# Last scan layer: D*x moved from TensorE to VectorE, three steps reordered, activation functions applied to whole tiles

## The chip, the cores and the metric

The kernel runs on one core of one Trainium2 chip. Its time is the device time of one execution in microseconds (us); the median over several executions counts. Engines are named as the profile names them: PE (TensorE, matmuls), PEld (its weight loads), DVE (VectorE), ACT (ScalarE), POOL (GpSimd) and SP (SyncE, which issues the DMAs).

## What is computed

Four layers of selective scans ("Mamba") over images of 48 x 48 tokens with 192 channels, batch 4, and an MLP at the end. Only the last layer's scans change. The reference computes one scan in these lines:

```python
xz = jnp.einsum('nld,ed->nle', x, W_in)
xi, z = (xz[..., :di], xz[..., di:])
xc = conv_b + sum((xp[:, k:k + L, :] * conv_w[:, k] for k in range(K)))
xc = _silu(xc)
dbc = jnp.einsum('nld,ed->nle', xc, W_x)
dt = jax.nn.softplus(jnp.einsum('nlr,dr->nld', dbc[..., :dr], W_dt) + b_dt)
def step(h, inp):
    dt_t, B_t, C_t, x_t = inp
    h = jnp.exp(dt_t[:, :, None] * A) * h + (dt_t * x_t)[:, :, None] * B_t[:, None, :]
    return (h, jnp.einsum('nds,ns->nd', h, C_t))
...
y = jnp.swapaxes(ys, 0, 1) + D * xc
y = y * _silu(z)
return jnp.einsum('nld,od->nlo', y, W_out)
```

There are 384 inner channels (`di`) and 16 states (`ds`). The layer scans along the rows and along the columns of each image, each way forward and backward. All numbers are fp32.

## The kernel before

**Jobs, blocks, groups.** The last layer is 96 jobs (`RowJob`) in 48 pairs. A pair treats the same 384 tokens: the forward job first, then its twin, the backward job. A job has 3 blocks of 128 channels, a block has 4 groups of 4 states, so a job has 12 groups, and a pair 24. `run_jobs` walks over all 1152 groups in one loop; what it issues for one group `t` is called slot `t` here. Slots F0 to F11 are those in which the forward job is scanned, B0 to B11 those of the backward job. While a job is scanned, the next one is prepared: in F0 to F11 the backward twin, in B0 to B11 the forward job of the next pair.

**One group.** ScalarE makes four decays `a` by exponentials (`decay`, two groups ahead; the buffers of `a` are three). VectorE multiplies `du` by B for two of the four states (tile `inputs`), scans these two, and then scans the other two, whose inputs `made` TensorE has produced (`fill`, six products of the turned `du`, called `duT`, with diagonals that a DMA brings). There is one `made` tile, so the next `fill` can't begin before this second scan ends. POOL multiplies `h` by C (`weigh`), and TensorE, two groups later, sums the four states of `h` over the groups with transposing matmuls into the PSUM tile `y`, of which there is one (`reduce`). The order on TensorE, VectorE, ScalarE and POOL is the order of issue in the loop.

**Once per block.** POOL makes `dus` = delta * x (`drive`); TensorE turns it over (`turn`, two groups ahead of the block) and ScalarE copies the result to `duT`; ScalarE also copies `dus` to the PSUM tile `du` (`enter`, ahead of the last of four exponentials). When the block's sum is complete, ScalarE copies it to `yT` (`take`, three groups after the block's last), TensorE turns it back into a `ps` tile on top of the product diagD*x (`turn_back`, four groups after), ScalarE copies that to `yt`, and POOL multiplies it by the gate `z`. `take` therefore falls in slots 2, 6 and 10, `turn` too, `turn_back` in slots 3, 7 and 11, and `drive` in slots 1, 5 and 9.

**Preparing the next job.** `units` gives a list of units, each of a TensorE part and a ScalarE part, with the slots in which these are issued; `Stream.run` takes them in order, and the TensorE parts at most two ahead. For a forward job (in B slots): three input projections (0 to 2), three convolutions (3 to 5; each takes two `ps` tiles), the x-projection `bc` (6), whose result ScalarE copies to `bcd` and SP sends to DRAM and back as broadcasts (`spread`, `fetch`) and as diagonals `dg` by scattered writes, the deltas (8) and the gates z (9 to 11). For a backward job (in F slots): convolutions (0 to 2), `bc` (4), the deltas (6), and the output products of the pair before (7 to 10); where a prior result is added, POOL's addition and the store follow in slot 11. All these go through the pool `ps`, which has two PSUM tiles.

ScalarE holds one set of function tables at a time. Silu, softplus and the exponentials are in different sets here, so each change of function puts an ACT_TABLE_LOAD into its queue. Copies and additions of a bias need none.

Of the kernel before, what the change touches and what calls it, by code (L numbers as in the profile page):

```python
# [13 lines left out]
AF = mybir.ActivationFunctionType  # L14
ALU = mybir.AluOpType
# [7 lines left out]
CH = 384  # L23
# [307 lines left out]
class ScanJob:  # L331
# [16 lines left out]
    def turn_back(self, i):  # L348
        pass
# [29 lines left out]
    def projections(self, xs, *slots):  # L379

        k, nc, w, pools = self.k, self.k.nc, self.w, self.pools
        nr = 2 * N + w.rank
        W = pools.W

        def bc(px):
            self.bcd = k.tile(pools.two, [nr, W], "bcd", 1)
            if self.entry is not None:
                k.g.memset(self.bcd[:, self.entry : self.entry + 1], 0.0)
            k.copy(self.bcd[:, self.tokens], px)
            self.spread()  # L390

        def delta(i):
            def act(pd):
                if i == 0:
                    self.delta = k.tile(pools.two, [128, 3, CH], "delta")
                k.act(self.delta[:, i, :], pd, AF.Softplus, bias=w.dtb[:, i, :])

            return self.unit(
                slots[1],
                128,  # L400
                lambda ps: (ps, [(w.dtT[2 * N : nr, i, :], self.bcd[2 * N : nr, self.tokens])]),
                act,
            )

        first = self.unit(
            slots[0],
            nr,
            lambda ps: (ps, [(w.xpT[:, i, :], xs()[: pools.wide, i, :]) for i in range(3)]),
            bc,
        )  # L410
        return first, [delta(i) for i in range(3)]

    def spread(self):

        self.bc = self.k.dram([2 * N, self.pools.W], "bc")
        self.k.nc.sync.dma_start(self.bc, self.bcd[: 2 * N, :])

    def fetch(self, g):

# [111 lines left out]
class DirJob(ScanJob):  # L531
# [20 lines left out]
    def units(self, last):  # L552
        bc, deltas = self.projections(lambda: self.xs, (1, 1), (2, 2))
        return [bc, *deltas]
# [12 lines left out]
    def gate(self, i):  # L567

        self.ys = self.k.tile(self.pools.ps, [128, 512], "ps")[:64, :CH]
        self.k.mmo(self.ys, [(self.pools.sum, self.yc)])  # L570
# [186 lines left out]
class RowJob(MambaJob):  # L757
# [55 lines left out]
        self.duT[i] = k.tile(pools.two, [128, CH], "duT")  # L813
        k.copy(self.duT[i], ps)

    def turned_over(self, out, of, start=True):

        for b in range(3):
            at = slice(b * 128, (b + 1) * 128)
            ins = self.k.t.matmul(  # L820
                out[:, at],
                of[:, at],
                self.k.ident,
                start=start,
                stop=True,
                is_transpose=True,
                skip_group_check=True,
            )
        return ins
# [76 lines left out]
    def turn_back(self, i):  # L906

        k = self.k
        back = k.tile(self.pools.ps, [128, 512], "ps")[:, :CH]
        k.t.matmul(  # L910
            back,
            self.w.diagD[:, i, :],
            self.xs[:, i, :],
            start=True,
            stop=False,
            skip_group_check=True,
        )
        self.turned_over(back, self.turned, False)
        if i == 0:
            self.yt = k.tile(self.pools.one, [128, 3, CH], "yt", self.pools.yts)  # L920
        k.copy(self.yt[:, i, :], back)

    def convolved(self, step, *slots):

        k, pools, w = self.k, self.pools, self.w
        made = []
        both = [(n % 3, n // 3) for n in (2 * step, 2 * step + 1)]
        offs = [(w.taps - 1) + (w.taps - 1 - t) * (1 if self.rev else -1) for t in range(w.taps)]

        def pe():  # L930
            made.extend(k.tile(pools.ps, [128, 512], "ps")[:, :HALF] for _ in both)
            for t, off in enumerate(offs):
                for r in range(4):
                    rows = slice(r * 32, (r + 1) * 32)
                    for (i, n), ps in zip(both, made):
                        c = (r + i) % 4
                        x = self.xh[rows, i, n * RC // 2 : (n + 1) * RC // 2, off : off + S]
                        k.t.matmul(
                            self.shaped(ps[c * 32 : (c + 1) * 32]),
                            w.diag[rows, i, t, :],  # L940
                            x,
                            start=t == 0,
                            stop=t == w.taps - 1,
                        )

        def act():
            if step == 0:
                self.xs = k.tile(pools.two, [128, 3, CH], "xc", 3)
            for (i, n), ps in zip(both, made):
                at = slice(n * HALF, (n + 1) * HALF)  # L950
                k.act(self.xs[:, i, at], ps, AF.Identity, bias=w.cb[:, i, :])
            if step == 2:
                k.act(self.xs, self.xs, AF.Silu)

        return slots, pe, act

    def units(self, last):
        k, w, two = self.k, self.w, self.pools.two
        halo = w.taps - 1

        def project(e):
            return [(w.inT[:, m, e * 128 : (e + 1) * 128], self.u[:, m, :]) for m in range(2)]

        def inner(i, slot):
            return self.unit(
                (slot, slot),
                128,
                lambda ps: (ps, project(i)),
                lambda ps: k.copy(self.part(i, halo), self.shaped(ps)),
            )  # L970

        def gate(i, *slots):
            def act(ps):
                if i == 0:
                    self.z = k.tile(two, [128, 3, CH], "z")
                k.act(self.z[:, i, :], ps, AF.Silu)

            return self.unit(slots, 128, lambda ps: (ps, project(3 + i)), act)

        if self.twin is not None:  # L980
            self.z = self.twin.z
            outputs = last.outputs((7, 7), (8, 8), (9, 9), (10, 10), (11, 11)) if last else []
            bc, deltas = self.projections(lambda: self.xs, (4, 4), (6, 6))
            return [
                *(self.convolved(n, n, n) for n in range(3)),
                bc,
                *deltas,
                *outputs,
            ]
        bc, deltas = self.projections(lambda: self.xs, (6, 6), (8, 8))  # L990
        return [
            *(inner(n, n) for n in range(3)),
            *(self.convolved(n, 3 + n, 3 + n) for n in range(3)),
            bc,
            *deltas,
            gate(0, 9, 10),
            gate(1, 10, 10),
            gate(2, 11, 11),
        ]

    def outputs(self, *slots):
        k = self.k
# [106 lines left out]
def run_jobs(jobs, side=None):  # L1109
# [2 lines left out]


    behind = 2 if jobs[0].pools.rows else 1
    ahead, taken, gated, driven = 2, behind + 1, behind + 2, 3
    last_group = jobs[0].pools.groups - 1
    groups = [(job, i, g) for job in jobs for i in range(3) for g in range(last_group + 1)]
    per = len(groups) // len(jobs)
# [1 line left out]
    def at_group(t, g):  # L1120

        if 0 <= t < len(groups) and groups[t][2] == g:
            return groups[t][:2]
# [18 lines left out]
    for t in range(len(groups) + gated + 1):  # L1142
        n, at = divmod(t, per)
        if at == 0:
            last = jobs[n - 1] if n else None
# [7 lines left out]
        if t < len(groups):  # L1153
            job, i, g = groups[t]
            job.scan(i, g)
        coming = at_group(t + 1, 0)
        if t + ahead < len(groups):
            job, i, g = groups[t + ahead]
            job.decay(i, g, (lambda: coming[0].enter(coming[1])) if coming else None)
        if done := at_group(t - gated - 1, last_group):  # L1160
            done[0].close(done[1])
        if done := at_group(t - taken, last_group):
            done[0].take(done[1])
        if t < len(groups):
            if t + 1 < len(groups):
                job, i, g = groups[t + 1]
                job.carry(i, g)
            job, i, g = groups[t]
# [19 lines left out]
        if 0 <= t - behind < len(groups):  # L1188
            job, i, g = groups[t - behind]
            job.reduce(i, g)  # L1190
        if t + 1 < len(groups):
            job, i, g = groups[t + 1]
# [39 lines left out]
class MambaWeights(Weights):  # L1232
    def __init__(self, k, pool, inT, xpT, dtT, vec, tag):
        super().__init__(k, pool, 128, 12, xpT, dtT, vec, tag)
        self.k, self.pool, self.in_src = k, pool, inT
        self.D = self.vec[:, :, 17:18]
        self.cb = self.vec[:, :, 18:19]
        self.taps = vec.shape[1] - 19
        self.diagD = k.tile(pool, [128, 3, 128], f"diagD{tag}")
        self.unit = k.strip if self.taps == 4 else k.ident  # L1240
        self.diag = k.tile(pool, [128, 3, self.taps, self.unit.shape[1]], f"diag{tag}")

# [2 lines left out]

    def diagonals(self, i):

        self.scaled(self.diagD[:, i, :], self.k.ident, self.D[:, i, :])
        for t in range(self.taps):
            self.scaled(self.diag[:, i, t, :], self.unit, self.vec[:, i, 19 + t : 20 + t])  # L1250

# [979 lines left out]
```

## Time and profile before

| | us |
|---|---|
| median of 3 runs | 19079.52 |
| lowest, highest | 19050.35, 19124.85 |
| the profiled execution | 19116.63 |
| its span | 19114.80 |
| of it, the last layer's groups (12893 to 18655) | 5762 |

Busy in these 5762 us: PE 5321, DVE 5001, POOL 4592, ACT 4265, PEld 4318. Mean granted clock 0.98.

A group of the profile is a set of like instructions: engine, operation, output tile <- input tiles, partitions x elements, count, then busy us in total, mean ns of one, and the idle time ahead of them with what ended it. A wait row reads: who waited, for whom, us in total, times, longest. A timeline row gives start and duration in us, and in brackets the idle time ahead. Nearly all instructions of the scans carry line 59, which is a helper's; they are told apart by their tiles. Matmuls are counted in passes, two for an fp32 product, so `ps<-xc,diagD` x2 is one product.

### The profile page before, as it was taken

Reading aid. Unit: us, or ns where it says so; the run is one execution under the profiler, and the core shown is the slowest. Engines: PE = TensorE matmul, PEld = TensorE weight load, DVE = VectorE, ACT = ScalarE, POOL = GpSimd, SP = SyncE. Lnnn points to the kernel's source line nnn. Section 1 sums busy time; section 2 is a strip of 40 time slices with the busy share of each in tenths; the row PEclk is TensorE's granted clock in tenths of the full one; section 3 lists DMA queues with packets and bytes.
Section 4 is the critical chain, followed back from the end, with each engine's and each line's share of the span. In section 5 each row is a group of like instructions: output and inputs, shape, how many; then the busy total and the mean of one; then the engine's idle time right before and its main releaser. Section 6 shows DMA issues by size and latency. Waiting matters only on the chain. (4 is left out here: it accounts for less than half of the span.)

```text
span 19114.8 us, 243541 instructions
## 1 busy us (share of the span) xinstructions
PE 16743.5 (88%) x85680; PEld 9426.4 (49%) x85680; DVE 17183.8 (90%) x8452; ACT 13342.8 (70%) x24116; POOL 14745.6 (77%) x10861
## 2 busy tenths in 40 slices
PE   8999999999998877777877877879999999999999
PEld 4545545444444422222222222237777777777774
DVE  9999999999999599999999999968888888888883
ACT  6767767666665466777777777767777777777773
POOL 7888888878877188888888888858778787777780
PEclk9999999999999977888777788789999999999999
DMA  3333333323232266666666666653333333333331
GB/s 112 123 112 118 117 117 119 115 104 120 104 112 101 80 137 143 152 144 152 146 152 152 145 148 142 146 135 112 113 113 113 113 114 115 115 109 112 114 111 47
DMA packets 864867, 2316.13 MB, mean 121 GB/s; under 512 B 390520, under 2 KB 648160, under 8 KB 711200
## 3 DMA queue, kind: packets, MB, share of 16 engines
q1 hardware_dynamic: 863648, 2300.55, 43.3%
q8 instruction: 683, 11.19, 0.2%
q14 instruction: 536, 4.39, 0.1%
HBM read 2104.78 MB, written 196.65 MB: 120 GB/s over the span
## 5 line engine op out<-in xcount | busy, mean ns | idle before, releaser
L59 POOL TENSOR_TENSOR h<-h,bcb 128x1536 f32<-128x1536 f32 x3456 | 11916.5, 3448 | 1370.1 <-DVE h L59 919.4
L59 DVE TENSOR_TENSOR_SCAN h<-a,inputs 128x1540 f32<-128x1540 f32 (+1 forms) x3456 | 9764.1, 2825 | 146.7 <-DVE inputs L59 2.3
L104 ACT ACTIVATE a<-delta,A 128x384 f32<-128x384 f32 (+1 forms) x13824 | 7443.5, 602 | 1791.9 <-DVE h L59 1771.2
L59 DVE TENSOR_TENSOR inputs<-du,bcb 128x1540 f32<-128x1540 f32 (+1 forms) x3456 | 5185.7, 1500 | 463.2 <-ACT a L104 119.8
L59 PE MATMUL y<-h,ident 128*128 128x384 f32 x9216 | 3362.8, 511 | 131.0 <-POOL h L59 129.0
L59 PE MATMUL y<-h,sum 128*64 128x384 f32 x9216 | 2689.0, 647 | 730.9 <-POOL h L59 528.3
L59 PEld LDWEIGHTS y<-h,ident 128*128 128x128 f32 x9216 | 1796.3, 199 | 1605.0 <-POOL h L59 315.0
L59 DVE TENSOR_TENSOR_SCAN h<-a,made 128x768 f32<-128x768 f32 x1152 | 2005.3, 1741 | 637.6 <-PE made L59 637.1
L59 POOL COPY state<-h 128x4 f32<-128x4 f32 x2304 | 431.6, 187 | 1967.2 <-DVE h L59 1943.0
L59 PEld LDWEIGHTS y<-h,sum 128*64 128x64 f32 x9216 | 856.7, 168 | 2164.0 <-issue 977.2
L59 PE MATMUL made<-bcb,duT 128*128 128x128 f32 x13824 | 1797.7, 281 | 113.3 <-DVE h L59 110.2
L59 PE MATMUL y<-ident,h 128*128 128x128 f32 x13824 | 1787.1, 281 | 58.3 <-ACT yT L104 55.6
L59 PEld LDWEIGHTS made<-bcb,duT 128*128 128x128 f32 x13824 | 1682.7, 197 | 161.6 <-DVE h L59 157.5
L59 PEld LDWEIGHTS y<-ident,h 128*128 128x128 f32 x13824 | 1601.1, 145 | 305.3 <-issue 155.6
L59 PE MATMUL ps<-bcd,dtT 12*128 12x384 f32 (+1 forms) x2304 | 1122.6, 602 | 318.4 <-ACT delta L104 315.3
L59 PE MATMUL ps<-u,inT 96*128 96x384 f32 x3456 | 1266.4, 494 | 144.6 <-ACT z L104 100.7
L59 PE MATMUL ps<-xh,diag 32*32 32x192 f32 (+1 forms) x20160 | 1088.7, 339 | 140.7 <-ACT xc L104 131.7
L104 ACT ACT_TABLE_LOAD x793 | 1017.4, 1283 | 13.3
L101 ACT ACT_TABLE_LOAD x788 | 1011.0, 1283 | 14.2 <-PEq L2221 0.7
L59 PEld LDWEIGHTS ps<-u,inT 96*128 96x128 f32 x3456 | 633.7, 192 | 573.2 <-ACT z L104 159.2
L59 PEld LDWEIGHTS ps<-bcd,dtT 12*128 12x128 f32 (+1 forms) x2304 | 429.2, 213 | 924.9 <-ACT delta L104 559.5
L59 PEld LDWEIGHTS ps<-xh,diag 32*32 32x32 f32 (+1 forms) x20160 | 647.6, 110 | 478.8 <-ACT xc L104 190.1
(151 smaller groups left out, 14510.8 us busy)
## 6 DMA issues: line engine op xcount, KB each, us to landing
bcb<-bc SPq DMA_DIRECT2D x384, 1540.0 KB
bcb<-bc SPq DMA_DIRECT2D x768, 770.0 KB
bcb<-bc SPq DMA_DIRECT2D x384, 1152.0 KB
bcb<-dg SPq DMA_DIRECT2D x384, 384.0 KB
y<-o SPq DMA_DIRECT2D x192, 288.0 KB
xs<-xi_wh SPq DMA_DIRECT2D x96, 288.0 KB
xs<-xi_hw SPq DMA_DIRECT2D x96, 288.0 KB
added<-y SPq DMA_DIRECT2D x96, 288.0 KB
```

Of the source, the lines that this page charges most:

```text
L59: return lambda *a, **kw: self.tc.keep_in_program_order(op(*a, **kw))
L101: self.in_order(self.nc.scalar.preload_act_table_set(LOG_EXP))
L104: return self.in_order(self.nc.scalar.activation(out, in_, func, **kw))
```

## The change

- `turn_back` no longer multiplies by `diagD`; VectorE adds D*x while it takes the turned sum from PSUM, in place of ScalarE's copy. `diagD` isn't made for this layer.
- `drive` comes one slot earlier: `driven` is 4 in place of 3 (slots 0, 4, 8).
- `take` is issued ahead of `decay`'s exponentials instead of after them.
- The x-projection of a forward job moves from slot 6 to 7, the first gate's copy from 10 to 9, and the addition of the output from 11 to 10.
- The gates z are copied as they come, and one Silu over the three blocks follows in slot 2 of the forward job's run (after the twin's own Silu).
- The deltas are copied with their bias, and one softplus over the three blocks follows.

Layers before the last keep their code paths: `behind` is 1 there.

```diff
@@ delta (in projections): the activation becomes a method
+                lambda ps: self.softplus(i, ps),
...
@@ RowJob.turn_back
         back = k.tile(self.pools.ps, [128, 512], "ps")[:, :CH]
-        k.t.matmul(
-            back,
-            self.w.diagD[:, i, :],
-            self.xs[:, i, :],
-            start=True,
-            stop=False,
-            skip_group_check=True,
-        )
-        self.turned_over(back, self.turned, False)
+        self.turned_over(back, self.turned)
         if i == 0:
             self.yt = k.tile(self.pools.one, [128, 3, CH], "yt", self.pools.yts)
-        k.copy(self.yt[:, i, :], back)
+        k.v.scalar_tensor_tensor(
+            self.yt[:, i, :], self.xs[:, i, :], self.w.D[:, i, :], back, ALU.mult, ALU.add
+        )
@@ RowJob.convolved
             if step == 2:
                 k.act(self.xs, self.xs, AF.Silu)
+                if self.twin is not None:
+                    k.act(self.z, self.z, AF.Silu)
@@ RowJob.units
-                k.act(self.z[:, i, :], ps, AF.Silu)
+                k.copy(self.z[:, i, :], ps)
...
-            outputs = last.outputs((7, 7), (8, 8), (9, 9), (10, 10), (11, 11)) if last else []
+            outputs = last.outputs((7, 7), (8, 8), (9, 9), (10, 10), (10, 10)) if last else []
...
-        bc, deltas = self.projections(lambda: self.xs, (6, 6), (8, 8))
+        bc, deltas = self.projections(lambda: self.xs, (7, 7), (8, 8))
...
-            gate(0, 9, 10),
+            gate(0, 9, 9),
...
+    def softplus(self, i, pd):
+        k = self.k
+        if i == 0:
+            self.delta = k.tile(self.pools.two, [128, 3, CH], "delta")
+        k.act(self.delta[:, i, :], pd, AF.Identity, bias=self.w.dtb[:, i, :])
+        if i == 2:
+            k.act(self.delta, self.delta, AF.Softplus)
@@ run_jobs
-    ahead, taken, gated, driven = 2, behind + 1, behind + 2, 3
+    ahead, taken, gated, driven = 2, behind + 1, behind + 2, 2 + behind
...
             job.scan(i, g)
+        if behind == 2 and (done := at_group(t - taken, last_group)):
+            done[0].take(done[1])
         coming = at_group(t + 1, 0)
...
-        if done := at_group(t - taken, last_group):
+        if behind == 1 and (done := at_group(t - taken, last_group)):
             done[0].take(done[1])
```

More of the change, by code (lines that the diff above doesn't have):

```diff
@@ L392, in delta @@
         def delta(i):
[L393 to L396, printed above, removed]
             return self.unit(
@@ L401, in delta @@
                 lambda ps: (ps, [(w.dtT[2 * N : nr, i, :], self.bcd[2 * N : nr, self.tokens])]),
-                act,
+                lambda ps: self.softplus(i, ps),
             )
@@ L416, in spread @@
         self.k.nc.sync.dma_start(self.bc, self.bcd[: 2 * N, :])
+    def softplus(self, i, pd):
+        if i == 0:
+            self.delta = self.k.tile(self.pools.two, [128, 3, CH], "delta")
+        self.k.act(self.delta[:, i, :], pd, AF.Softplus, bias=self.w.dtb[:, i, :])
     def fetch(self, g):
@@ L814, in turn, with turned_over @@
         k.copy(self.duT[i], ps)
-    def turned_over(self, out, of, start=True):
+    def turned_over(self, out, of):
         for b in range(3):
@@ L823, in turned_over @@
                 self.k.ident,
-                start=start,
+                start=True,
                 stop=True,
@@ L999, in units, with softplus @@
         ]
+    def softplus(self, i, pd):
+        k = self.k
+        if i == 0:
+            self.delta = k.tile(self.pools.two, [128, 3, CH], "delta")
+        k.act(self.delta[:, i, :], pd, AF.Identity, bias=self.w.dtb[:, i, :])
+        if i == 2:
+            k.act(self.delta, self.delta, AF.Softplus)
     def outputs(self, *slots):
@@ L1238, in __init__ @@
         self.taps = vec.shape[1] - 19
-        self.diagD = k.tile(pool, [128, 3, 128], f"diagD{tag}")
+        if self.taps != 4:
+            self.diagD = k.tile(pool, [128, 3, 128], f"diagD{tag}")
         self.unit = k.strip if self.taps == 4 else k.ident
@@ L1246, in diagonals @@
     def diagonals(self, i):
-        self.scaled(self.diagD[:, i, :], self.k.ident, self.D[:, i, :])
+        if self.taps != 4:
+            self.scaled(self.diagD[:, i, :], self.k.ident, self.D[:, i, :])
         for t in range(self.taps):
```

## The prediction

> **What bounds the kernel now.** I read the 40 slices of the page first (the last layer is the stretch where PE and DVE are both high), then stretches, groups and waits in its steady part (13862 to 17686 us), then its timeline. All edits lie in the last layer, whose groups run from 12893 to 18655 us: 5762 us, 1152 groups, 48 pairs of jobs.
>
> A steady stretch (us; PE, PEld, DVE, ACT, POOL busy; clock; DMA):
> ```profile
> 14818.00:15296.00 478.00, 445.12 (x4332) 360.17 (x4332) 418.29 (x290) 358.45 (x652) 380.70 (x193) 0.98 0.37 113
> ```
> PE is busy 93% of it, DVE 88%, POOL 80%, ACT 75%. Two engines so near full in a loop mean that neither bounds it alone. Groups and waits of 13862 to 17686 us (31.8 pairs):
> ```profile
> L59 PE MATMUL ps<-xc,diagD 128*128 128x384 f32 x382 | 155.2, 488 | 0.0
> L104 ACT ACTIVATE yt<-ps 128x384 f32<-128x384 f32 x191 | 92.0, 482 | 106.0 <-PE ps L59 106.0
> L101 ACT ACT_TABLE_LOAD x190 | 243.8, 1283 | 3.3
> L104 ACT ACT_TABLE_LOAD x190 | 243.8, 1283 | 2.9
> ...
> DVE h L59 <- PE made L59: 427.1, 385, 3.9
> PE ps L59 <- POOL dus L59: 125.0, 109, 2.8
> DVE inputs L59 <- ACT du L104: 41.8, 32, 1.4
> ```
> The first wait carries the case: VectorE stands 427.1/31.8 = 13.4 us a pair before its second scan, waiting for TensorE's `made`. TensorE itself loses 3.9 us a pair waiting for `dus`; twelve table loads a pair sit on ScalarE. The timeline of slots B2 to B4 (PE, then DVE, then ACT; start, us):
> ```profile
> 15044.59 1.55 PE L59 MATMUL ps<-xh,diag 32*32 32x192 f32 x64
> 15046.88 0.55 PE L59 MATMUL ps<-ident,dus 128*128 128x128 f32 x3 [0.74 <-POOL dus L59]
> ...
> 15049.91 0.81 PE L59 MATMUL ps<-xc,diagD 128*128 128x384 f32 x2
> 15050.56 0.49 PE L59 MATMUL ps<-ident,yT 128*128 128x128 f32 x3
> 15050.11 1.75 DVE L59 TENSOR_TENSOR_SCAN h<-a,made 128x768 f32<-128x768 f32 x1 [0.76 <-PE made L59]
> 15053.15 0.96 DVE L59 TENSOR_TENSOR inputs<-du,bcb 128x768 f32<-128x768 f32 x1 [1.29 <-ACT du L104]
> 15048.27 1.17 ACT L104 ACTIVATE xc<-xc 128x1152 f32<-128x1152 f32 x1
> 15049.34 0.47 ACT L104 ACTIVATE duT<-ps 128x384 f32<-128x384 f32 x1
> 15049.83 1.28 ACT L101 ACT_TABLE_LOAD   x1
> 15051.13 1.61 ACT L104 ACTIVATE a<-delta,A 128x376 f32<-128x376 f32 x3
> 15052.64 0.47 ACT L104 ACTIVATE du<-dus 128x384 f32<-128x384 f32 x1
> ```
> The reader sees `dus` hold TensorE, hence `made` hold VectorE, and a second chain on ScalarE (Silu, duT, load, exponentials, du) hold the next multiplication.
>
> **The bookkeeping.** An unhindered group takes VectorE 4.32 us (15055.82 to 15060.14). The 24 slots of a pair, averaged from the timeline over 36 pairs, take 120.26 us against 24 x 4.32 = 103.7. The surplus of 16.6 lies in B3 (2.1), B4 (1.6), B7 (2.8), B9 (1.5), B11 (0.9), F0 (0.6), F3 (2.3), F7 (1.9), F8 (1.2), F9 to F11 (1.2) and crumbs. Two rules from the code and the timeline explain it: fill(t+1) starts at the later of TensorE's being through with slot t and the end of the second scan of t; that scan starts at the later of fill's end and the first scan's end. Start-to-start TensorE prices from the timeline: fill 1.40, reduction 1.34, convolution 1.47, x-projection 2.06, delta product 0.80 each, inT 1.29, outT 1.93, turn 0.38, turn back 0.33, diagD 0.65. With the waits for ACT and POOL put in as their queues order them, the two rules give 118.2 a pair and nearly the same slots. The 2.1 us left over lie where reductions and fills run at half speed behind the delta products.
>
> **What the Trainium skill says.** "ScalarE: Activation LUTs", What ACT_TABLE_LOAD costs: 1283 ns a load plus a drain of some 1380. The trace has the 1283; no drain shows (15049.83 + 1.28, and the exponential starts at 15051.13). "VectorE: DVE Perf Modes", Why PSUM operands drop a tier: fp32 with a PSUM operand is held to one element a cycle; the nearest row, quoted below, agrees in kind. "TensorE: Matmul & The Clock Gate", What's actually happening: a monitor halves TensorE's clock after too little activity. The trace agrees: a reduction of 2.77 us at 15067.35 against 1.47, and mean clocks of 0.96 to 0.99. "Perfetto Trace Analysis", Matmuls: groups should rotate PSUM banks so that emptying one overlaps the next; here `ps` has two tiles, and step 4 turns on it.
>
> **The change, part by part (a pair).**
> 1. diagD gone: 6 x 0.65 = 3.9 us of TensorE, all in slots with a turn back.
> 2. The D*x instruction on VectorE, 6 times, each on its path. Nearest row, of the MLP:
> ```profile
> L2016 DVE SCALAR_TENSOR_TENSOR mo<-mop,mb,macc 96x384 f32<-96x384 f32 x48 | 29.5, 614 | 118.9 <-PE mop L139 118.9
> ```
> I take 0.61 (bounds: 0.47, the MLP's 96x384 TENSOR_SCALAR, and 0.95, its 96x768 TENSOR_TENSOR with a PSUM operand): +3.7 us. It needs no wait of its own: the turn back follows fill(t) directly, the second scan takes 1.7 us. ScalarE loses 6 x 0.48 us of `yt` copies.
> 3. `dus` a slot earlier (POOL: h, dus, h in place of h, h, dus). The turn finds it ready: TensorE gets 3.9 us back, in B2, B10, F2 (ahead of the surplus of B3, B11, F3). POOL's next weighing comes 1.0 us later; its reduction is two slots off, and POOL is at 80%. For the first block, `dus` now follows the delta in slot B8 itself: softplus ends about with POOL's weighing, 0 to 1 us.
> 4. New waits, from emptying by VectorE. In B3 the convolution takes both `ps` tiles; one is the turned sum, free only after the second scan and D*x. Then fill to fill takes 0.6 + 1.7 + 1.47 + 1.34 + 1.40 = 6.5, which leaves B4 at about 6.15 (now 5.90); in the other five turn-back slots the next unit uses the other tile.
> 5. `yT` ahead of the exponentials, and the projection from B6 to B7: the 1.2 us wait for `yT` and the crowd in B6 (projection, turn) go. B7 falls from 7.1 to 4.9, B8 stays at 4.3. Exponentials start 0.47 later, two slots ahead of use. SP's chain moves with it: bc and be stores, 8 diagonal scatters (6.43 us), first fetches, issued by 15017.5 for a fill at 15034.6. Five us later they still land in time: nothing.
> 6. One Silu over z, one softplus over delta: four loads fewer (5.1 us of ScalarE, B9 to B11, off the path), but the Silu of z (1.16, as xc's) lies in F2 and the longer softplus (load 1.28 + 1.16) in F6, both ahead of `du`. Carried through ScalarE's queue, VectorE waits for `du` 1.6 us in F3 and 1.1 in F7, against 1.3 now in F3. F3 becomes 6.8 (6.6), F7 6.3 (6.2). F8 falls to the floor.
> 7. The output's addition (1.8 us of POOL, half the pairs) in slot 10, away from the gate of 11: SP's wait for it (89.7 us in all) comes earlier, ahead of a fetch needed three slots on. Nothing.
>
> Sum: floor 103.7 + D*x 3.7 + B4 1.8 + `du` 2.7 + waits for `made` in B9 (after the delta products) 0.8, F11 0.4, F3 and F7 0.5 + crumbs 0.2 = 113.8. The same rules gave 118.2 for the kernel before. Half speed: 2.1 stays with the delta products, and I add 0.2 for TensorE's 3 us wait in B3: 116.1. That is 4.2 us a pair, 48 x 4.2 = **200 us**, and 19116.6 - 200 = 18917 for the profiled execution. That lies 37 above the median of 19079.5; against the median, **18880**.
>
> **The rivals.**
> - *Half speed grows* (0.17). For: TensorE idles longer at a time (3.0 us in B3, 1.7 and 1.6 ahead of F6's delta products). Against: waits of 1.6 to 2.2 in B2 leave the next matmuls at full speed. Two further slow windows of 3.4 us a pair, half of each on the path and half its work lost, cost 2 us: gain 2.2, 18975.
> - *VectorE alone bounds* (0.08). If `du` and the tile of B3 hide: 103.7 + 3.7 + crumbs 1.9 = 109.3, 11 us a pair, 18555. For: 13.4 us of waiting for TensorE, which loses 7.8 of work and waits. Against: ScalarE's chain is already late by 1.3 in F3.
> - *Slower: the two `ps` tiles* (0.06). If what stands behind each turn back has to wait as in B4, the six slots take 6.6: 103.7 + 13.7 + `du` 2.7 + B9 0.8 + half speed 2.1 = 123.0, +132 us, 19210. Each such slot costs 1.7 beyond my sum, so three of the five more decide. Against: one tile is enough for xpT, outT and inT.
> - *The relief isn't there* (0.03): the new order in the program already lacks diagD and moves `dus`, so only equal waits elsewhere give 19080.
>
> **How the numbers follow.** My case has 0.66, with 18810 to 18950 (D*x 0.47 to 0.95, half speed 1 to 3). The range of 18770 to 19020 adds most of the first rival. Within 0.5% is 95 us, about what a measurement of this kernel can tell: faster 0.66 + 0.08 + half of 0.17 = 0.83, same 0.11, slower 0.06.
>
> **What would show it.** Right: no PE wait for `dus`; DVE's wait for `made` down from 13.4 to 3 to 5 us a pair; DVE's wait for `du` up from 1.3 to near 2.7; PE waiting some 3 us before the convolution of B3; eight loads a pair; D*x near 0.61. Wrong: D*x over 1 us, DVE waiting for `ps` before D*x, the clock in the layer below 0.96, or DVE waiting for loads of `bcb`.

## The result and the profile after

| | before | after |
|---|---|---|
| median of 6 runs each, us | 19085.22 | 18950.75 |
| lowest, highest | 19050.35, 19124.85 | 18899.59, 18975.79 |
| the profiled execution, and its span | 19116.63, 19114.80 | 18975.79, 18974.0 |
| the last layer's groups in it | 5762 | 5606 |
| a pair, mean of 36 | 120.26 | 116.84 |

The ratio is **0.9924 [0.9904 to 0.9944]**: faster by 0.76%, 134 us between the medians. The last layer accounts for it: 156 us in the profiled executions, and 3.42 us x 48 pairs = 164. (The layers ahead of it ended 15.7 us later in that execution of after, at 12909.4 against 12893.7; their code is the same.)

The same steady stretch of after (us; PE, PEld, DVE, ACT, POOL busy with counts; granted clock, 1.00 being full speed; DMA share; GB/s):

```profile
14818.00:15296.00 478.00, 442.50 (x4351) 361.29 (x4350) 437.23 (x321) 344.54 (x633) 390.34 (x197) 0.98 0.35 113
```

VectorE is now busy 437.2 of 478 us, 91% where it was 88%, and TensorE still 93%. Two engines near full remain two engines near full. Groups and waits of 13862 to 17686 us, which hold 32.7 pairs of after:

```profile
L59 DVE SCALAR_TENSOR_TENSOR yt<-xc,vec,ps 128x384 f32<-128x384 f32 x196 | 115.4, 589 | 0.0
L104 ACT ACTIVATE delta<-delta 128x1152 f32<-128x1152 f32 x65 | 75.7, 1164 | 0.7
L104 ACT ACTIVATE z<-z 128x1152 f32<-128x1152 f32 x32 | 36.8, 1149 | 0.0
L104 ACT ACT_TABLE_LOAD x130 | 166.8, 1283 | 2.3
L101 ACT ACT_TABLE_LOAD x130 | 166.8, 1283 | 2.3
```

```profile
DVE h L59 <- PE made L59: 210.2, 182, 3.4
DVE inputs L59 <- ACT du L104: 86.0, 49, 2.0
PE ps L59 <- DVE yt L59: 81.0, 33, 2.5
PE y L59 <- ACT yT L104: 20.0, 33, 0.6
```

D*x takes 589 ns, and VectorE never idles ahead of it (the 0.0 at the end of its row). The table loads are 260, eight a pair. VectorE's wait for `made` has halved, from 13.4 to 210.2/32.7 = 6.4 us a pair; TensorE's wait for `dus` is gone from the list. In their place stand the wait for `du` (86.0/32.7 = 2.6 us) and one long wait a pair, TensorE's for the `ps` tile that VectorE empties in `yt` (81.0/33 = 2.46 us each). That one is where the prediction's size failed. TensorE in B3 and B4 of one pair, then VectorE (start, us, what; in brackets the idle time ahead and what ended it):

```profile
15087.31 0.49 PE L59 MATMUL ps<-ident,yT 128*128 128x128 f32 x3
15087.73 0.51 PE L59 MATMUL ps<-xh,diag 32*32 32x192 f32 x2
15090.69 2.03 PE L59 MATMUL ps<-xh,diag 32*32 32x192 f32 x62 [2.46 <-DVE yt L59]
15092.66 2.65 PE L59 MATMUL y<-ident,h 128*128 128x128 f32 x12
15095.15 1.50 PE L59 MATMUL made<-bcb,duT 128*128 128x128 f32 x12
15096.58 1.54 PE L59 MATMUL ps<-xh,diag 32*32 32x192 f32 x64
15098.05 1.53 PE L59 MATMUL y<-ident,h 128*128 128x128 f32 x12
```

```profile
15088.41 1.73 DVE L59 TENSOR_TENSOR_SCAN h<-a,made 128x768 f32<-128x768 f32 x1
15090.05 0.59 DVE L59 SCALAR_TENSOR_TENSOR yt<-xc,vec,ps 128x384 f32<-128x384 f32 x1
...
15091.56 1.75 DVE L59 TENSOR_TENSOR_SCAN h<-a,inputs 128x768 f32<-128x768 f32 x1
15096.69 1.75 DVE L59 TENSOR_TENSOR_SCAN h<-a,made 128x768 f32<-128x768 f32 x1 [3.37 <-PE made L59]
```

The turned sum lies complete in PSUM at 15087.8, but VectorE is inside a slot: it ends its scan at 15090.1, then takes the sum, and only then has the convolution its second tile. When TensorE resumes, the same work takes longer: the 62 convolution matmuls 2.03 us where the next block's 64 take 1.54, the reduction 2.65 where the next takes 1.53. The granted clock of the wait and of what follows, cut where the clock changes (columns as above):

```profile
15088.18:15091.58 3.40, 0.94 (x47) 0.86 (x50) 3.37 (x5) 0.00 (x0) 2.52 (x2) 1.00 0.00 0
15091.59:15094.99 3.40, 3.40 (x41) 2.77 (x26) 1.72 (x1) 2.22 (x6) 3.09 (x2) 0.50 0.02 5
15095.00:15098.40 3.40, 3.40 (x82) 2.91 (x81) 1.71 (x2) 0.67 (x2) 0.00 (x0) 1.00 0.00 0
```

TensorE is busy for 0.94 us of the first 3.4; through the next 3.4 it is busy without a gap, but at half speed; then it is at full speed again. In the 33 such places of the stretch the convolution takes 2.16 us on average (27 times over 1.8) and the reduction behind it 2.49 (24 times over 2). The clock record of the trace (the granted clock over time, from which that column is averaged) has one stretch of 3.41 us at half speed behind the wait in all 33: it begins 0.03 to 1.31 us after the convolution resumes, and where it begins late it falls on the reduction and the fill. Convolution, reduction and fill together take 5.93 to 5.96 us in all 33. So VectorE stands 3.37 us before its second scan of B4.

The other new chain, the one on ScalarE in slots F2 and F3, as ScalarE and then VectorE have it:

```profile
15029.20 1.17 ACT L104 ACTIVATE xc<-xc 128x1152 f32<-128x1152 f32 x1
15030.27 1.15 ACT L104 ACTIVATE z<-z 128x1152 f32<-128x1152 f32 x1
15031.32 0.47 ACT L104 ACTIVATE duT<-ps 128x384 f32<-128x384 f32 x1
15031.81 1.28 ACT L101 ACT_TABLE_LOAD   x1
15033.11 1.61 ACT L104 ACTIVATE a<-delta,A 128x376 f32<-128x376 f32 x3
15034.62 0.47 ACT L104 ACTIVATE du<-dus 128x384 f32<-128x384 f32 x1
```

```profile
15032.60 0.59 DVE L59 SCALAR_TENSOR_TENSOR yt<-xc,vec,ps 128x384 f32<-128x384 f32 x1
15035.13 0.96 DVE L59 TENSOR_TENSOR inputs<-du,bcb 128x768 f32<-128x768 f32 x1 [1.95 <-ACT du L104]
```

The Silu over z stands in the queue ahead of `du`, and VectorE waits 1.95 us for it. Slot by slot (us, averages over 36 pairs; "predicted" as stated there or worked out from its terms; those left out moved by 0.2 at most):

| slot | before | predicted | after |
|---|---|---|---|
| B3 | 6.40 | 4.9 | 4.82 |
| B4 | 5.90 | 6.15 | **7.80** |
| B7 | 7.13 | 4.9 | 4.82 |
| B8 | 4.32 | 4.3 | 4.75 |
| B9 | 5.78 | 5.1 | 5.62 |
| B11 | 5.27 | 4.9 | 4.82 |
| F0 | 4.92 | | 4.39 |
| F3 | 6.59 | 6.8 | 6.93 |
| F7 | 6.23 | 6.3 | 6.72 |
| F8 | 5.56 | 4.3 | 4.36 |

### The profile page after: what moved, and what is told of

Same layout as the page of the kernel before. It is cut to its first block, busy times and chain, and to the rows that moved or that the text cites. A ratio compares the mean times of both kernels' runs of the same rounds, so it can differ in the third digit from the quotient of the medians.

```text
span 18974.0 us, 241933 instructions
## 1 busy us (share of the span) xinstructions
PE 16565.9 (87%) x85104; PEld 9331.9 (49%) x85104; DVE 17300.8 (91%) x8734; ACT 13128.5 (69%) x23783; POOL 14756.3 (78%) x10861
## 5 line engine op out<-in xcount | busy, mean ns | idle before, releaser
L59 PE MATMUL y<-ident,h 128*128 128x128 f32 x13824 | 1802.1, 282 | 32.7 <-ACT yT L104 28.4
L104 ACT ACTIVATE delta<-ps,vec 128x384 f32<-128x384 f32 x1152 | 643.9, 580 | 456.7 <-PE ps L59 446.4
L104 ACT ACTIVATE xc<-ps,vec 128x192 f32<-128x192 f32 (+1 forms) x864 | 368.2, 471 | 807.7 <-PE ps L59 806.4
```

What stands on the lines that cost most here:

```text
L59: return lambda *a, **kw: self.tc.keep_in_program_order(op(*a, **kw))
L104: return self.in_order(self.nc.scalar.activation(out, in_, func, **kw))
```

## The experiments

All ratios are against the kernel before, with 95% intervals; the pair times come from each kernel's own profiled execution and its waits from 13862 to 17686 us of it, which is 31 to 34 pairs. The theory: the gain comes from the order (`dus`, `yT`), and D*x on VectorE costs more than it brings as long as B3 needs both `ps` tiles. The rival: the relief of TensorE by `diagD` is what pays.

**1. D*x back on TensorE** (label e1_dx_on_pe), everything else as in after:

```diff
-        self.turned_over(back, self.turned)
+        k.t.matmul(back, self.w.diagD[:, i, :], self.xs[:, i, :], start=True, stop=False, ...)
+        self.turned_over(back, self.turned, False)
-        k.v.scalar_tensor_tensor(self.yt[:, i, :], self.xs[:, i, :], self.w.D[:, i, :], back, ...)
+        k.copy(self.yt[:, i, :], back)
```

> The changed kernel with D*x back on TensorE (the diagD product under the turned sum, ScalarE's copy to yt); all else as changed. Theory 1 (order): the gain came from the earlier dus, the earlier yT and the grouped functions, and D*x on VectorE costs more than it saves, by 6 x 0.59 us on VectorE's path and by the wait for the ps tile in B3 with the half speed behind it. Then a pair takes about 114.8 us against 116.84 in the changed kernel, 100 us less in all: some 18850, ratio to the kernel before near 0.987. Theory 2 (relief): TensorE is the bound and the missing diagD is the gain; then putting 3.9 us a pair back costs up to 190 us, and the time is 19040 to 19140, ratio 0.998 to 1.003.

Measured: 18851.65 us, **0.9875 [0.9859 to 0.9890]**, a pair 114.66. That is better than after, whose interval it does not touch: the part that gives the change its name costs about 0.5% inside it. B4 falls from 7.80 to 5.03 us. A group and the waits of VectorE:

```profile
L59 PE MATMUL ps<-xc,diagD 128*128 128x384 f32 x400 | 162.2, 487 | 0.0
```

```profile
DVE h L59 <- PE made L59: 191.5, 277, 2.4
DVE inputs L59 <- ACT du L104: 123.5, 100, 2.5
```

TensorE has `diagD` again, 162.2 us, and VectorE's wait for `made` is not larger in sum (191.5 against 210.2). But the sum hides an exchange. In after 111 of the 210.2 us lie in B4 (33 times some 3.37), here 20. In all other slots the wait is 99 us in after and 171 here, 3.0 against 5.1 us a pair: without `diagD` TensorE does deliver earlier. What VectorE pays for it is larger: six times 0.59 us, and the wait in B4. The wait for `du` is larger here too, with ScalarE's copies to `yt` back: it is the next thing to be late.

**2. D*x on VectorE alone** (e2_dx_alone), on the kernel before: edit 1 reversed, and nothing else.

> The kernel before with D*x on VectorE alone (no diagD product, no copy by ScalarE); nothing else of the change. Theory 1 (order): nothing gained; what TensorE saves is covered by its wait for dus and by the new wait for the ps tile in B3: 117.9 us a pair by the trace's durations, against 118.2 for the kernel before, and half speed on the convolution of B3 on top; 0 to +80 us, ratio 1.000 to 1.004. Theory 2 (relief): 3.9 us a pair, 190 us, go: 18900, ratio 0.990.

Measured: 19162.87 us, **1.0034 [1.0021 to 1.0047]**, a pair 121.75: slower, by 64 us. VectorE's and TensorE's waits:

```profile
DVE h L59 <- PE made L59: 402.7, 316, 3.9
PE ps L59 <- POOL dus L59: 136.6, 107, 2.3
PE ps L59 <- DVE yt L59: 50.7, 32, 1.6
```

TensorE waits for `dus` as in the kernel before, and the wait for `yt` comes on top. B4 is 7.29 us here. With experiment 1, from both sides: D*x on VectorE does not pay in either order of the work.

**3. `dus` late again** (e3_dus_late):

```diff
-    ahead, taken, gated, driven = 2, behind + 1, behind + 2, 2 + behind
+    ahead, taken, gated, driven = 2, behind + 1, behind + 2, 3
```

> The changed kernel with drive one slot later again (driven = 3). Theory 1: TensorE waits for dus again at the turns, 1.5 to 2.4 us each in F2, B2, B6 and B10, VectorE behind it about 1 us in each next slot; 3.8 us a pair back, 180 us: 19130, ratio 1.002. Rival: with diagD gone TensorE has room for the wait, and little comes back: 18950 to 19000.

Measured: 19192.71 us, **1.0051 [1.0032 to 1.0070]**, a pair 122.08, slower than expected. Without this one digit the whole change is a loss. TensorE's wait came back longer than it was in the kernel before (125.0):

```profile
PE ps L59 <- POOL dus L59: 224.9, 185, 2.2
```

**4. Functions by block** (e4_by_block): Silu on each z as it is copied (with the first gate's copy in slot 10), softplus on each delta, as before.

```diff
-        k.act(self.delta[:, i, :], pd, AF.Identity, bias=self.w.dtb[:, i, :])
-        if i == 2:
-            k.act(self.delta, self.delta, AF.Softplus)
+        k.act(self.delta[:, i, :], pd, AF.Softplus, bias=self.w.dtb[:, i, :])
```

> The changed kernel with Silu of z and softplus of delta applied block by block as in the kernel before (first gate in slots 9 and 10). Twelve table loads a pair again. Theory 1: the loads of B9 to B11 hold ps tiles and delay du and duT, and TensorE's third delta product waits for a table: 1.5 us a pair back in spite of shorter du chains in F3 and F7; 70 us: 19020, ratio 0.997. Rival a: the loads are off the path and the grouping's longer chain ahead of du (2.76 us of DVE wait a pair) is the larger: 18820 to 18880. Rival b: no difference.

Measured: 18990.94 us, 0.9941 [0.9925 to 0.9956], a pair 117.81. The interval overlaps that of after, so the times alone don't separate the two; the slots show the exchange that was expected in kind. F3 and F7 fall from 6.93 and 6.72 to 5.99 and 5.61 us, and B9 and B11 rise from 5.62 and 4.82 to 6.59 and 6.54. Grouping is about even, as far as these times can tell.

**5. TensorE kept busy in its wait** (e5_busy_wait): twelve needless transposes into unused columns of the same tile, behind the turn back of B3.

```diff
+        if i == 2 and self.twin is None:
+            for _ in range(12):
+                k.t.matmul(whole[:, CH:], k.ident, k.ident, start=True, stop=True, is_transpose=True, ...)
```

> The changed kernel with 12 transposes of the identity, into unused columns of the ps tile, behind the turn back in B3 (needless work, about 1.3 us of TensorE once a pair). In the changed kernel TensorE stands about 2.5 to 3.0 us there, and the convolution and reduction behind take 2.01 and 2.41 us in place of 1.47 and 1.37. Theory: the idle time itself lets the clock fall to half; filled to less than 1.7 us idle, both go back to full speed, 1.6 us a pair, 75 us less: about 18875, slot B4 6.2 in place of 7.8. Rival: the slowness comes from the pair of tiles or from VectorE's reading, and the time stays or grows by what the transposes add: 18950 to 19010.

Measured: 18903.91 us, 0.9909 [0.9895 to 0.9922], a pair 116.11. The interval overlaps that of after; what the run shows lies in its slots and its clock. B4 is 6.19 us, as expected, where it was 7.80. TensorE in B3 and B4, then busy times and granted clock of the wait and of the convolution with its reduction:

```profile
15039.27 0.49 PE L59 MATMUL ps<-ident,yT 128*128 128x128 f32 x3
15039.59 1.47 PE L59 MATMUL ps<-ident 128*128 128x128 f32 x12
15041.00 0.51 PE L59 MATMUL ps<-xh,diag 32*32 32x192 f32 x2
15042.65 1.54 PE L59 MATMUL ps<-xh,diag 32*32 32x192 f32 x62 [1.15 <-DVE yt L59]
15044.12 1.53 PE L59 MATMUL y<-ident,h 128*128 128x128 f32 x12
```

```profile
15039.20:15042.60 3.40, 2.31 (x20) 1.76 (x18) 3.40 (x4) 0.57 (x2) 2.54 (x2) 1.00 0.00 0
15042.60:15047.00 4.40, 4.35 (x94) 3.90 (x102) 2.64 (x2) 2.72 (x6) 4.04 (x2) 1.00 0.01 4
```

TensorE did more work and its next work was faster: 1.54 and 1.53 us at a clock of 1.00, in all 33 places. That settles that the idle time, not the tile's arrival itself, made B4 dear by its last 1.6 us. But less than half of it, 0.73 us a pair, reached the end. B9 rises from 5.62 to 6.28: the reduction that follows the delta products takes over 2 us in 22 of 33 places, in after only in 3 of 32. There the clock is low: TensorE in B8 and B9 of this kernel, and the stretch from that reduction on, granted 0.62 (in after, the same place from 15117.2 to 15120 us has 1.00):

```profile
15065.13 2.49 PE L59 MATMUL ps<-bcd,dtT 12*128 12x384 f32 x6
15067.55 2.77 PE L59 MATMUL y<-ident,h 128*128 128x128 f32 x12
```

```profile
15067.50:15072.00 4.50, 4.50 (x26) 4.46 (x26) 2.13 (x2) 4.30 (x4) 4.07 (x2) 0.62 0.70 163
```

That this comes from the change in B3 is not shown. The clock record has half speed beginning behind the delta products of B8 in 9 of 32 places of after and 22 of 33 here, but also in 9 of 34 in run 6, which has none in B3 either, and in 19 of 33 in run 7, which has it in B3.

**6. Convolutions one slot later** (e6_conv_later), so that B3's turn back has a tile to itself:

```diff
-            *(self.convolved(n, 3 + n, 3 + n) for n in range(3)),
+            *(self.convolved(n, 4 + n, 4 + n) for n in range(3)),
```

> The changed kernel with the forward job's three convolutions in slots 4 to 6 in place of 3 to 5, so that none of them stands behind a turn back; D*x stays on VectorE. Theory 1 (the tile): the wait of 2.5 us for yt goes, and with it the half speed behind it: B4 falls from 7.8 to 4.4, B7 rises to 5.6 (convolution and turn in B6): 112.4 us by durations plus 1 to 2 of half speed, 3 us a pair, 150 us less: 18800, ratio 0.985. Rival: the work is only moved, B6 and B7 take what B3 and B4 lose: 18930 to 18970.

Measured: 18775.3 us, **0.9842 [0.9827 to 0.9856]**, a pair 113.47. B4 is at 4.32, the time of an unhindered group. The wait for `yt` is gone from TensorE's list and VectorE's wait for `made` is a third of after's 210.2; the one for `du` is now the larger:

```profile
DVE inputs L59 <- ACT du L104: 123.1, 87, 2.0
DVE h L59 <- PE made L59: 67.8, 118, 1.9
```

One digit in the list of units, on top of the change, gives about as much as the whole change did (0.9924 to 0.9842).

**7. `du` ahead of the exponentials** (e7_du_first), in the last layer:

```diff
-            if j == NG - 1 and between is not None:
+            if j == (0 if pools.rows else NG - 1) and between is not None:
```

> The changed kernel with the copy of dus to du ahead of all four exponentials of its slot, in place of after three. Theory (ScalarE's chain): the chain Silu, Silu, duT, load, three exponentials, du is 1.5 us shorter, VectorE's waits for du (86 us in 13862 to 17686, 2.6 a pair) go nearly away, F3 falls from 6.9 to 5.2 and F7 from 6.7 to 5.3, and 1.1 of the 2.7 us comes back in F9 to F11 as waits for made: 1.6 us a pair, 75 us: 18875. Rival: made ends those slots as well, nothing: 18950.

Measured: 18847.33 us, **0.9872 [0.9856 to 0.9887]**, a pair 114.76. VectorE waits for `du` no more; F3 and F7 come to 4.88 and 5.36. Its one wait left:

```profile
DVE h L59 <- PE made L59: 226.6, 264, 3.4
```

**8. `yT` after the exponentials** (e8_take_late): `take` at its old place.

> The changed kernel with take after the exponentials again. Theory 1: yT lies behind four exponentials, and behind Silu and its loads in B6: TensorE's reduction waits there 2 to 4 us for the y tile; B7 rises from 4.8 to 7.4: 3.3 us a pair, 160 us: 19110, ratio 1.001. Rival: the earlier bc of B6 was the crowd, and it is gone (bc is in B7): under 40 us.

Measured: 19156.23 us, **1.0043 [1.0030 to 1.0056]**, a pair 122.08: 5.2 us above after, where I had expected 3.3. TensorE waits for `yT` up to 4.0 us: the copy stands behind Silu, its loads and four exponentials in ScalarE's queue, and the projection that stood in B6 and filled part of this time now lies in B7. The clock record has half speed behind this wait too, in all 31 places. B7 takes 9.78 us:

```profile
PE y L59 <- ACT yT L104: 153.6, 62, 4.0
```

**9. Edits 6 and 7 together** (c1_both), D*x on VectorE.

> The changed kernel with both: convolutions in slots 4 to 6, and du copied ahead of the exponentials; D*x on VectorE. If the two gains lie in different slots (B3, B4 and F3, F7) they add: 176 us and 104 us below the changed kernel, 18670. If TensorE's total sets a floor, less: by the trace's durations 110.8 us a pair, plus 1 to 2 of half speed, 18700. Not below 18560, which is VectorE's own 107.3 us a pair.

Measured: **18699.52 us, 0.9793 [0.9777 to 0.9808]**, a pair 111.38: faster than both kernels. VectorE's only wait, and the whole stretch of 3824 us:

```profile
DVE h L59 <- PE made L59: 120.8, 238, 2.4
```

```profile
13862.00:17686.00 3824.00, 3635.10 (x36633) 2989.02 (x36632) 3660.55 (x2674) 2909.72 (x5318) 3297.66 (x1663) 0.99 0.39 122
```

VectorE is busy 3660.55 of 3824, 96%, TensorE 95%. VectorE's own work in a pair is 24 x 4.32 + 6 x 0.59 = 107.2, so 4.2 us a pair are left above it; 120.8/34.3 = 3.5 of them are this wait, 1.8 in B9 alone.

**10. The same with D*x on TensorE** (c2_both_pe).

> The same as the run before it, with D*x back on TensorE (diagD product, ScalarE's copy). With the wait of B3 gone and du early, D*x on VectorE has only its own 6 x 0.59 us to set against 6 x 0.65 us of TensorE. Theory: the two are even (110.8 us a pair by durations for both), within 20 us of each other. Rival: VectorE is the tighter one now, and this is faster by up to 6 x 0.59 = 3.5 us a pair, 170 us; or TensorE is, and it is slower by up to 190.

Measured: 18700.23 us, 0.9793 [0.9777 to 0.9810], a pair 111.88. Even:

```profile
DVE h L59 <- PE made L59: 227.1, 288, 2.4
```

With `diagD` back VectorE waits 227.1/34.2 = 6.6 us a pair for `made`, against 3.5 in run 9: 3.1 us more, for the 3.5 us that D*x takes from VectorE. Once B3 has its tile and `du` is in time, it makes no difference here on which of the two engines D*x runs.

**11. Two convolutions in B4** (c3_two_in_b4), on top of run 9, to relieve the slot of the delta products:

```diff
-            *(self.convolved(n, 4 + n, 4 + n) for n in range(3)),
+            *(self.convolved(n, (4, 4, 5)[n], (4, 4, 5)[n]) for n in range(3)),
```

> As the first of these three (D*x on VectorE, du first), with the convolutions in slots 4, 4 and 5, so that the last of them is not in the slot of the turn (B6). Expected by durations 0.5 us a pair less, 24 us. Rival: the second convolution in B4 waits for ScalarE to empty the first one's tiles, and it is slower by up to 1.5 us a pair, 70 us.

Measured: 18715.44 us, 0.9805 [0.9788 to 0.9822], a pair 112.70: the wrong way, though the interval overlaps that of run 9. B5 takes 5.38 us, and TensorE has a new wait, for ScalarE's convolved x (41.5 us in the stretch); VectorE's for `made` rises to 160.7.

## Why the prediction came out as it did

The direction and the range were right, and so were the places of the waits. The size was too large: 200 us predicted, 134 measured between the medians (156 in the layer), and a pair took 116.84 where the sum gave 116.1. The median of 18950.75 lies at the end of the case that I held likeliest (18810 to 18950) and nearer to the 18975 of the first rival than to 18880.

- **Step 1 and the first wait.** "The first wait carries the case" held: the wait for `made` was what the change shortened. It fell to 6.4 us a pair, not 3 to 5, and the excess lies in B4, which has 3.4 of it. The relief by `diagD` is real, 3.1 us a pair between runs 9 and 10, but step 2 takes as much back. With B4's wait the two together are a loss in this order of the work, of 0.5% (run 1), and alone, on the kernel before, of 0.34% (run 2).
- **Step 2**, 0.61 us for D*x: 0.589 measured, with no wait of its own.
- **Step 3**, TensorE's wait for `dus` gone: shown, and run 3 prices it at 1.3% of the whole (1.0051 against 0.9924). This and step 5 are the change's gain. (These are prices of taking one part out of the new order; they don't add up to the 0.76%.)
- **Step 4**, the convolution of B3 waits for the tile: shown, 2.46 us in the bracket plus the two matmuls ahead of it. **The term that was mis-sized stands here: "I add 0.2 for TensorE's 3 us wait in B3".** B4 took 7.80 in place of 6.15, so the wait cost 1.65 more: about half of the 3.41 us at half speed that follow it in every pair. Run 5 shows that the idle time is the cause: with it filled, B4 is 6.19. The first rival named this mechanism and argued against it from waits of 1.6 to 2.2 us that "leave the next matmuls at full speed" in B2. The trace of before had the answer in the same slot: from 13862 to 17686 us the first 17 of its waits for `dus` in B2 are 1.63 to 1.65 us long, and none is followed by half speed; the other 15 are 2.80 to 2.84 us, and all 15 are:

```profile
16062.44 0.90 PE L59 MATMUL ps<-ident,dus 128*128 128x128 f32 x3 [2.82 <-POOL dus L59]
16063.13 2.76 PE L59 MATMUL y<-ident,h 128*128 128x128 f32 x12
```

  In run 2 the wait in B3 is 1.6 us, and the convolution takes over 1.8 us in 18 of 32 places.
- **"2.1 stays with the delta products"** failed too, in the other direction. Outside half speed the sum had 113.8; the 3.0 us above it lie in B4 (1.65), B9 (0.48), B8 and F7 (0.42 each), so at most 1.3 with the delta products. That takes back half of the error in B4: 0.7 us a pair is left, 36 us in 48 pairs, and the sum came so near by luck in part. Half speed grew little in all. From 13862 to 17686 us the clock record of before has 5.6 us of it a pair, 15 stretches behind the wait in B2 and 33 behind delta products; that of after has 6.1 us, 33 stretches behind the wait in B3 and 25 behind delta products. The sum left out those of B2, which went with the wait for `dus`.
- **Step 5**: the wait for `yT` is 0.6 us, B7 4.82 (4.9 predicted). Run 8 prices it at 1.2%. That B7 would be this dear with `take` late wasn't seen.
- **Step 6**: 2.7 us of waiting for `du` predicted, 2.6 measured; F3 and F8 within 0.13, F7 0.42 over. That grouping is about even by itself (run 4) was not worked out: the gain at B9 and B11 is given back at F3 and F7.
- **The rivals.** "The two `ps` tiles" as a general loss is out: in after only B3's turn back waits. "VectorE alone bounds" comes near in run 9 (VectorE 96% busy, TensorE 95%), not in after.
- **A slip of the reading.** The timeline that the prediction gives as B2 to B4 is that of F2 to F4: the convolution in front of the turn, the Silu over xc and the wait for `du` belong there. No term of the sum hangs on the label.

Where half speed falls can be read from the clock record. In each of the 13 traces every stretch at half speed begins on one grid of 3.413 us (in after all 542, to within 1 ns). This agrees with "TensorE: Matmul & The Clock Gate", What's actually happening, which speaks of free-running windows of 3413 ns. In B3 the stretch came at the first or second step of the grid after the wait began, in every pair, so the 6 of 33 convolutions that took under 1.8 us had escaped nothing: their half speed fell on the reduction and the fill. The delta products of B8 and F6, 2.49 us of products whose contraction is 12 rows, were followed by half speed when they began 0.0 to 1.2 us into a step, so that nearly all of them lay inside it (25 of 25 in after, 36 of 36 in run 5), and not when they began elsewhere (0 of 40 and 0 of 30). So the 22 of 33 in B8 of run 5 against 9 of 32 in after go with where the pairs lay on the grid. Why the grid counts products of 12 rows as it does is not shown.

## What to carry to other kernels

Work moved from one nearly full engine to another brings what the waiting engine gains, less what the work costs it: here 3.1 against 3.5 us a pair. Ask first when the target engine can take it, and which tile stays occupied until then. When two buffers serve a loop, find the one slot that needs both and move that unit a slot away before moving any work. The cost of an idle TensorE is not its length alone: look at the granted clock and the durations of what follows, in all instances and not in one.

## What was not expected of the hardware

A wait of 2.46 us (3.4 us in which TensorE was busy 0.94) was followed in all 33 places by 3.41 us at half speed, in the middle of a stream in which TensorE is 93% busy; twelve needless matmuls in the gap (1.47 us) kept the clock at 1.00 there in all 33 places. Waits of 1.64 us in B2 of before were followed by none (0 of 17), those of 2.8 us always (15 of 15), and those of 2.16 us in B6 of run 3 always (31 of 31). Delta products, whose contraction is 12 rows, were followed by half speed although TensorE was busy without a gap (2.47 of 2.50 us), in B8 in 22 of 33 places of run 5 against 9 of 32 in after; what told the two apart was where on the grid of 3.413 us they began.
